# A four-layer attention and convolution kernel: symmetric layer 2 begins with its diagonal blocks, its closings are split into five parts, layer 1 is ticked at every step, end sums of layer 3 are recorded later

## The chip, the cores and the metric

The kernel runs on one core of a Trainium2 chip, as one program. The metric is the device time of one execution in microseconds (us). All data are fp32. The engines are named as in the profile: PE (TensorE matmul), PEld (its weight loads), DVE (VectorE), ACT (ScalarE), POOL (GpSimd), SP (SyncE, which here only issues DMAs).

## The reference, cut to what matters

The input x has shape (4, 64, 64, 64): four images of 64 by 64 pixels with 64 channels. Four layers follow one another, and every image passes all of them; only the normalisation at the end of layer 3 looks at all images together.

```python
x = L0(x)   # attention: softmax(q k^T) over 4096 tokens, out[n] = sum_m attn[m, n] v[m]; gamma * out + x
x = L1(x)   # layer norm, 64->256 pointwise, 3x3 depthwise, gate, mean over pixels, 128->64 pointwise, residual,
            # layer norm, 64->256 pointwise, gate, 128->64 pointwise, residual
x = L2(x)   # scores = X^T X over 4096 tokens (a symmetric matrix), softmax, product with X; + x
x = L3(x)   # attention with 32 inner channels, 1x1 projection, normalisation over all images; + x
```

## The kernel before, in words

**Layer 0** (`layer0`) has 32 items per image; an item is one tile of 128 tokens against all 4096. An item has four steps g. Each step records a score block (line 1090, eight matmul instructions), one exponential with its row sum on ACT (line 1095), and, six steps later (`LAG = 6`), a product block (line 1116, eight instructions). After step g = 0 of the next item `scale` (lines 1103 to 1106) makes the scaled weights `vq` on DVE that the products of the item need.

**Layer 1** (`layer1`, with `norm`) is a Python generator. Each `yield` hands back a number of lane microseconds; the class `Lane` advances its clock at every `tick` and records the generator's next part when the clock has passed what the parts before have asked for. So the layer's instructions are dealt out between the matmuls of other layers, and the order on every engine is the order in which they are recorded: PE, ACT, DVE and POOL keep that order strictly. There are two lanes, `conv` (layer 1) and `misc` (projections, closings, features). The depthwise convolution is 76 parts per image, nearly all DVE work (lines 1231 to 1244); the parts around it are matmuls (lines 1165, 1200, 1253, 1262, 1285) with ACT and DVE steps that wait for one another. Layer 1 of image b is handed to the lane at item 32 b + 34.

**Layer 2 of image 0** (`layer2`) has 32 items: four score blocks with exponentials (lines 1323, 1331), and one item later four product blocks (line 1341). `close2` scales the result and adds it to x (lines 1370 to 1377).

**Layer 2 of images 1 to 3** (`layer2s`) uses that the score matrix is symmetric. The 4096 tokens are cut into eight pieces of 512. Steps go over pairs (h, g) of pieces, 72 steps in all, two for each pair. A diagonal step (h = g, "own") has only a score block (line 1431), two exponentials (line 1436) and a product block (line 1481). Another step ("other") is also turned by DVE (line 1448, 32x32 block transposes), summed by POOL (line 1459), and, four turned steps at a time, multiplied again (`turned_products`, line 1497, 128 matmul instructions) and added to the accumulator `m.A` by DVE (line 1471). Step n is item n of the stage. A product block is recorded at least two items after its scores, none before item 4. The turned products of four steps follow two items after the last of them. `m.A` is allocated and cleared by POOL at one item. When the first half of the turned products of h = 6 has been recorded, `when_free` runs `keys3`, which copies the keys of layer 3 of the image before by 16 DMAs from SP (line 1620).

`close2s` finishes such an image: part 0 makes reciprocals of the sums (lines 1548 to 1554), then four parts each turn 1024 columns on PE (line 1559), scale them on DVE (line 1560) and add them to x (line 1566, two adds). It and `open3`, which makes the inputs of layer 3, run while the next image is in layer 2.

**Layer 3** (`layer3`) has 64 items in two halves of 32: scores (line 1641), two exponentials (line 1652), two items later products (line 1698) and a running sum of the exponentials in `m.tg`, two thirds on DVE (line 1689), one third by accumulating DMAs from POOL (line 1671, added at line 1691). `totals` sums over the partitions at the end of each half (matmul of line 1710), copies the sums (DVE, line 1734) and makes the reciprocals (ACT, lines 1718 and 1721, DVE lines 1726 to 1728).

**Order of stages.** Layer 0 of images 0 to 3 with layer 1 beside it, layer 2 of image 0, then for b = 1, 2, 3: layer 2 of image b (`layer2s(b)`) and layer 3 of image b - 1, and at the end layer 3 of image 3. The main loop `run` calls one item, ticks the lanes, runs what is due after this item (`at`), and ticks them again. Four slots of the PSUM tile `PS` are dealt out in turn; in `layer2s` three are, `new_ps()` each.

Of the kernel before, what the change touches and what calls it, by code (L numbers as in the profile page):

```python
# [691 lines left out]
def fast_path(ctx: ExitStack, tc: tile.TileContext, a: dict, out: bass.AP, bad):  # L692
# [387 lines left out]
    def layer0(b):  # L1080
        x, m = X[:, b], im[b]
        tiles = {}

        def score(t, g):
            es, _, zs = tiles[t]
            ps = new_ps()
            for c in range(2):
                for r in range(2):
                    rows_ = slice(64 * r, 64 * r + 64)
                    mm(  # L1090
                        ps[64 * c : 64 * c + 64, bass.ts(r, 512)],
                        m.q[rows_, 128 * t + 64 * c : 128 * t + 64 * c + 64],
                        x[rows_, bass.ts(g, 512)], start=True, stop=True,
                    )
            act(  # L1095
                es[g // 2][:, bass.ts(g % 2, 1024)], ps, AF.Exp, bias=SHIFT0,
                accum_out=zs[:, g : g + 1],
            )

        def scale(t):  # L1100
            _, vq, zs = tiles[t]
            tot = sums0[:, b, t : t + 1]
            nc.vector.tensor_reduce(tot, zs, AX.X, ALU.add)  # L1103
            rec = sm.tile([128, 1], F32, tag="rec", name="rec")
            nc.vector.reciprocal(rec, tot)
            nc.vector.tensor_scalar_mul(vq, m.v[:, t, :], rec)

        def product(t, i):
            if b == 0 and t == 0 and i == 0:
                take_slots(0, 1)  # L1110
            es, vq, _ = tiles[t]
            for s in range(2):
                for r in range(2):
                    j, rows_ = (i + 2 * r) % 4, slice(64 * r, 64 * r + 64)
                    k = 1024 * (j % 2) + 512 * s
                    ins = mm(  # L1116
                        PS[64 * s : 64 * s + 64, 2048 + 512 * j : 2560 + 512 * j], vq[rows_, :],
                        es[j // 2][rows_, k : k + 512],
                        start=t == 0 and i < 2, stop=t == 31 and i >= 2,
                    ).ins  # L1120
                    if s == r == 0 and len(steps) > 1:
                        wait_for(ins, steps[-2])
            steps.append(nc.gpsimd.nop(nofuse=True).ins)
            wait_for(steps[-1], ins)
            if t == 31 and i >= 2:
                for j in (i, i - 2) if b == B - 1 else (i - 2, i):
                    xs = x[:, bass.ts(j, 512)]
                    stt(xs, PS[:, 2048 + 512 * j : 2560 + 512 * j], gam0, xs, ALU.mult, ALU.add)
                if b == B - 1 and i == 3:
                    take_slots(0, 1, 2)  # L1130

        def item(t):
            tiles[t] = (
                [new_e() for _ in range(2)], sm.tile([128, C], F32, tag="vq", name="vq", bufs=4),
                sm.tile([128, 4], F32, tag="zs", name="zs", bufs=4),
            )
            for g in range(4):
                if g == 2 and between:
                    between.pop()()
                score(t, g)  # L1140
                late.append(lambda g=g: product(t, g))
                conv.tick(1.95)
                misc.tick(1.8)
                if g == 0 and t:
                    scale(t - 1)
                follow()
            if t == 31:
                scale(t)

        for t in range(32):  # L1150
            items.append((lambda t=t: item(t), 0.0))


    def norm(x, y):
# [2 lines left out]
        sq = [new_t("sq"), new_t("sq")]  # L1157
        for i in range(2):
            act(sq[i], x[:, bass.ts(i, 1024)], AF.Square)
        yield 3.0  # L1160
        ps = new_ps()
        for i, src in enumerate(((x, x), (sq[0], sq[1]))):
            for j in range(4):
# [30 lines left out]
    def layer1(b):  # L1194
# [53 lines left out]
                    yield 1.8  # L1248
        ytot = sm.tile([128, 1], F32, tag="ytot", name="ytot")
        nc.vector.tensor_reduce(ytot, ysum, AX.X, ALU.add)  # L1250
        yield 5.0
        ps = new_ps()
        mm(ps[:, 0:1], sca, ytot, start=True, stop=True)
        ch = sm.tile([128, 1], F32, tag="ch", name="ch")
# [18 lines left out]
        for j in range(4):  # L1273
            t, u = new_t(), new_t("u")
            for r in range(2):
# [3 lines left out]
                    act(t, ps, AF.Identity, bias=pwb[:, 1, 0:1])  # L1279
                else:  # L1280
                    stt(u, ps, pwb[:, 1, 1:2], t, ALU.add, ALU.mult)
                yield 4.0 if r else 3.0
            ps = new_ps()
            for s in range(2):
                mm(ps[64 * s : 64 * s + 64, 0:512], pw4, u[:, bass.ts(s, 512)], start=True, stop=True)
# [21 lines left out]
    def layer2(b):  # L1307
# [7 lines left out]
        def scores(n):  # L1315
# [3 lines left out]
            for jb in range(4 * (n % 8), 4 * (n % 8) + 4):  # L1319
# [10 lines left out]
                es[n, jb] = e[:, bass.ts(jb % 2, 1024)]  # L1330
                act(es[n, jb], ps, AF.Exp, bias=SHIFT2, accum_out=m.zs[:, jb, ib : ib + 1])  # L1331
                follow(0)

        def products(n):
            ib = n // 8
# [24 lines left out]
            )  # L1360

        for n in range(32):
            items.append((lambda n=n: scores(n), 4.6))
            at(first + n + (2 if n == 0 and b > 1 else 1), lambda n=n: products(n))
            if n % 8 == 7:
                at(first + n + 2, lambda n=n: turn(n // 8))
# [18 lines left out]
    def layer2s(b, when_free):  # L1385
# [2 lines left out]
        x, m, first = X[:, b], im[b], len(items)  # L1388
        xw = x.rearrange("p (w h) -> p w h", h=H)
        quads = ((0, 0), (1, 0), (0, 1), (1, 1))  # L1390
        m.zs = sm.tile([128, 144], F32, tag="zs2", name="zs2")
        m.cs = sm.tile([128, 128], F32, tag="cs2", name="cs2", bufs=1)
        used = {}
        steps = []
        for h in range(8):
            own = [(h, h, u, None, None) for u in range(2)]
            other = [
                (h, g, u, pi, 2 * gi + u)
                for pi, pair in enumerate(SIDES[h]) for gi, g in enumerate(sorted(pair)) for u in range(2)
            ]  # L1400
            steps += own + other if h < 6 else other + own
        st = {"e": {}, "T": {}, "esum": {}}

        def slot(g, t):
# [15 lines left out]
        def score(n):  # L1420
            h, g, u, pi, ti = steps[n]
            if n == 0:
                take_slots(0, 1, 2)
            if n % 2 == 0:
                st["pair"] = new_e()
            e = st["e"][n] = st["pair"][:, bass.ts(n % 2, 1024)]
# [34 lines left out]
                nc.gpsimd.tensor_add(esum[:, 0:512], esum[:, 0:512], esum[:, 512:1024])  # L1461

        def spread_sums(h):
            esum = st["esum"][h]
            nc.vector.transpose(esum[:, 512:1024], esum[:, 0:512])
            nc.vector.tensor_reduce(
# [22 lines left out]
        def turned_products(h, pi):  # L1489
            T, slots = st["T"][pi], [new_ps(), new_ps()]  # L1490
            for e in range(16):
                c = e % 2
                w = 1024 * (h % 2) + 256 * (e % 4) + 64 * (e // 4)
                for q in range(4):
# [3 lines left out]
                        slots[q // 2][64 * c : 64 * c + 64, o : o + 256], st["xr"][rows_, w : w + 64],  # L1498
                        T[rows_, bass.ts(e, 256)], start=e < 2, stop=e >= 14,
                    )  # L1500
            view = m.A.rearrange("p (g t q j) -> p g q t j", g=8, t=4, q=4)
            for i in range(2):
                for gi, g in enumerate(sorted(SIDES[h][pi])):
                    add_to(
                        view[:, g, 2 * i : 2 * i + 2],
                        slots[i].rearrange("p (q m) -> p q m", q=2)[:, :, 128 * gi : 128 * gi + 128]
                        .rearrange("p q (t j) -> p q t j", j=32),
                    )

        last_of = {}  # L1510
# [5 lines left out]
        def item(n):  # L1516
# [4 lines left out]
            turned(n)  # L1521
            column_sums(n)
            todo.append(n)
            if n == 6:
                m.A = new_big("A")
                nc.gpsimd.memset(m.A, 0.0)
            if n >= 4:
# [97 lines left out]
    def layer3(b):  # L1625
# [164 lines left out]
        for n in range(64):  # L1790
# [2 lines left out]
            if last and n == 63:  # L1793
                at(first + n + 2, close_last)
            elif n % 32 == 31:
                at(first + n + (2 if n == 63 and b < 2 else 4), lambda n=n: totals(n))
                at(first + n + 11, lambda n=n: close(n // 32))


# [10 lines left out]
    for b in range(B):  # L1810
# [4 lines left out]
            misc_from[f + 16] = [features2(b + 1)]  # L1815
        else:
            layer2s(b, lambda b=b: keys3(b - 1))
            misc_from[f + 3] = [close2(0) if b == 1 else close2s(b - 1)]
            misc_from[f + 28] = [open3(b - 1)]
            f = len(items)  # L1820
            misc_to[f] = True
            layer3(b - 1)
            if b + 1 < B:
                misc_from[f + 22] = [features2(b + 1)]
    f = len(items)

    def keys_of_last():
# [7 lines left out]
    def run():  # L1835
# [10 lines left out]
        for i in range(max(max(due) + 1, len(items))):  # L1846
# [7 lines left out]
            if i < len(items):  # L1854
                fn, us = items[i]
                fn()
            conv.tick(1.25 * us)
            misc.tick(us)
            for fn in due.get(i, []):
                fn()  # L1860
            conv.tick(1.25 * us)
            misc.tick(us)


# [183 lines left out]
```

## Time and profile before

| what | value |
| --- | --- |
| time, median of 3 runs | 2500.96 us (2496.73 to 2501.36) |
| time of the profiled execution | 2502.84 us |
| its span, first to last instruction | 2501.0 us |
| mean granted PE clock | 0.993 |
| PE busy | 2432.0 us (97%) |
| ACT busy | 1644.3 us (66%) |
| DVE busy | 1433.5 us (57%) |
| POOL busy | 506.7 us (20%) |

The stages as the trace shows them: layer 0 from about 18 to 1012 us; layer 2 of image 0 to about 1289 us; `layer2s(1)` to 1490 us, layer 3 of image 0 to 1629 us; `layer2s(2)` to 1832 us, layer 3 of image 1 to 1971 us; `layer2s(3)` to about 2175 us, and layer 3 of images 2 and 3 to about 2470 us; 31 us of output follow.

How to read it: the trace names each instruction by engine and source line. A timeline line gives start, duration, engine, line, operation, tiles, count, and in brackets the idle time before it with what ended it. A waits line reads "engine tile line <- releaser: us in total, times, longest us". A windows line gives a stretch, its length, busy us (instruction count) of PE, PEld, DVE, ACT and POOL, the granted PE clock, the DMA share and GB/s. Matmuls are pipelined, so a busy PE is not a PE at its peak: the number of instructions in a stretch says more than its busy time.

### The profile page before, as it was taken

The numbers are of one execution on the slowest core, as the hardware profiler recorded it, in microseconds if no ns is written. First come the engines' busy times: TensorE is split into PE (matmuls) and PEld (weight loads), VectorE is DVE, ScalarE is ACT, GpSimd is POOL, SyncE is SP. The second block draws the span as 40 slices with busy tenths as digits, with TensorE's granted clock in tenths as the row PEclk, the third lists the DMA queues.
The fourth block names the chain that finished last, engine by engine and source line by source line (L and its number), as shares of the span: only waits on it lengthen the run. The fifth ranks groups of instructions, "written<-read, shape, count | busy, mean of one in ns | idle before, by whom it ended". The sixth has DMA issues, their size and how long they took to land.

```text
span 2501.0 us, 62233 instructions
## 1 busy us (share of the span) xinstructions
PE 2432.0 (97%) x27037; PEld 937.0 (37%) x27037; DVE 1433.5 (57%) x1701; ACT 1644.3 (66%) x2975; POOL 506.7 (20%) x345
## 2 busy tenths in 40 slices
PE   9999999999999999999889999989999899999998
PEld 3343463334553446333224442134422245421113
DVE  2010267226652367258436657885668865687886
ACT  4666766666666776666554459944579744578996
POOL 2000000000000000000026651246731366511110
PEclk9999999999999999999999999999999999999999
DMA  3000000000000000010000017610066400275554
GB/s 78 1 18 1 18 1 18 18 18 2 18 1 18 18 18 1 18 18 18 18 18 19 19 45 152 136 27 19 19 128 128 85 19 21 60 152 119 119 119 120
DMA packets 59150, 115.33 MB, mean 46 GB/s; under 512 B 11148, under 2 KB 30325, under 8 KB 58869
## 3 DMA queue, kind: packets, MB, share of 16 engines
q0 software_dynamic: 19136, 67.68, 13.5%
q1 hardware_dynamic: 38981, 41.75, 7.5%
q8 instruction: 214, 3.51, 0.6%
q10 hardware_dynamic: 752, 1.85, 0.2%
q14 instruction: 67, 0.55, 0.1%
HBM read 4.80 MB, written 4.19 MB: 4 GB/s over the span
## 4 chain that ended last, share of the span: by engine, by line
PE 84%; DVE 9%; ACT 4%; DMA 1%; issue 1%; SPq 0%; DVEq 0%; POOL 0%; ACTq 0%; POOLq 0%
PE PS L1116 17%; PE PS L1090 17%; PE PS L1641 8%; PE PS L1431 7%; PE PS L1698 7%; PE PS L1481 7%; PE PS L1497 6%; DVE tg L1689 3%; PE PS L1341 3%; PE PS L1323 3%; PE PS L1200 2%; ACT e L1652 2%; DVE y L1233 2%; DMA xn<-e 1%; ACT e L1095 1%
## 5 line engine op out<-in xcount | busy, mean ns | idle before, releaser
L1095 ACT ACTIVATE e<-PS 128x1024 f32<-128x1024 f32 x512 | 523.7, 1023 | 326.3 <-PE PS L1090 285.4
L1116 PE MATMUL PS<-e,vq 64*64 64x512 f32 x4096 | 573.9, 591 | 0.0
L1090 PE MATMUL PS<-X,q 64*64 64x512 f32 x4096 | 571.4, 590 | 1.8 <-DVE X L974 1.7
L1652 ACT ACTIVATE e<-PS 128x512 f32<-128x512 f32 (+2 forms) x589 | 500.0, 919 | 53.0 <-PE PS L1641 29.9
L1436 ACT ACTIVATE e<-PS 128x512 f32<-128x512 f32 x432 | 253.6, 593 | 316.0 <-PE PS L1431 293.8
L1689 DVE TENSOR_TENSOR tg<-tg,e 128x2048 f32<-128x2048 f32 x174 | 398.5, 2290 | 51.7 <-ACT e L1652 39.8
L1459 POOL TENSOR_TENSOR esum<-e 128x1024 f32<-128x1024 f32 x21 | 49.7, 2367 | 1445.4 <-ACT e L1436 1445.4
L1233 DVE SCALAR_TENSOR_TENSOR y<-pad,vec,y 128x1024 f32<-128x1024 f32 x240 | 308.0, 1284 | 7.3
L1459 POOL TENSOR_TENSOR esum<-esum,e 128x1024 f32<-128x1024 f32 x126 | 299.1, 2374 | 52.3 <-ACT e L1436 44.9
L1641 PE MATMUL PS<-tg,ph 32*64 32x512 f32 x4096 | 299.2, 614 | 2.2 <-ACT e L1652 2.0
L1090 PEld LDWEIGHTS PS<-X,q 64*64 64x64 f32 x4096 | 195.0, 133 | 248.4 <-issue 166.0
L1116 PEld LDWEIGHTS PS<-e,vq 64*64 64x64 f32 x4096 | 195.3, 133 | 241.3 <-issue 141.3
L1698 PE MATMUL PS<-e,tg 128*32 128x512 f32 x2048 | 273.4, 606 | 0.0
L1448 DVE STREAM_TRANSPOSE turned<-e 128x1024 f32<-128x1024 f32 x168 | 206.6, 1239 | 69.4 <-ACT e L1436 69.2
L1431 PE MATMUL PS<-ko 64*64 64x512 f32 x1728 | 231.5, 601 | 3.9 <-DVE t L1560 3.9
L1481 PE MATMUL PS<-e,X 64*64 64x512 f32 x1728 | 223.6, 589 | 0.0
L1103 DVE TENSOR_REDUCE sums<-zs 128x1 f32<-128x4 f32 x128 | 19.8, 154 | 347.9 <-ACT e L1095 347.5
L1497 PE MATMUL PS<-turned,xn 32*64 32x256 f32 x5376 | 159.5, 381 | 15.1 <-DVE turned L1448 11.3
L1331 ACT ACTIVATE e<-PS 128x1024 f32<-128x1024 f32 x128 | 129.3, 1024 | 62.0 <-PE PS L1323 61.9
L1471 DVE TENSOR_TENSOR A<-PS,A 128x256 f32<-128x256 f32 (+1 forms) x216 | 92.4, 476 | 122.8 <-PE PS L1497 87.8
L1671 POOL DMA_DIRECT2D xn<-e x112 | 97.7, 910 | 291.1 <-ACT e L1652 208.5
L1641 PEld LDWEIGHTS PS<-tg,ph 32*64 32x64 f32 x4096 | 65.4, 130 | 224.2 <-ACT e L1652 174.5
(224 smaller groups left out, 1874.8 us busy)
## 6 DMA issues: line engine op xcount, KB each, us to landing
xn<-e POOLq DMA_DIRECT2D x128, 512.0 KB, 5.2
xn<-X SPq DMA_DIRECT2D x336, 32.0 KB
xn<-t SPq DMA_DIRECT2D x64, 128.0 KB
ph<-tg SPq DMA_DIRECT2D x64, 128.0 KB
ko<-ko SPq DMA_DIRECT2D x16, 256.0 KB
xr<-in_x_dram SPq DMA_DIRECT2D x13, 256.0 KB
q<-q SPq DMA_DIRECT2D x12, 256.0 KB
out_dram<-o SPq DMA_DIRECT2D x7, 256.0 KB
```

What stands on the lines that cost most here:

```text
L1090: mm(ps[64 * c : 64 * c + 64, bass.ts(r, 512)], m.q[rows_, 128 * t + 64 * c : 128 * t + 64 * c + 64], x[rows_, bass.ts(g, 512)], start=Tru ...
L1095: act(es[g // 2][:, bass.ts(g % 2, 1024)], ps, AF.Exp, bias=SHIFT0, accum_out=zs[:, g : g + 1],)
L1116: ins = mm(PS[64 * s : 64 * s + 64, 2048 + 512 * j : 2560 + 512 * j], vq[rows_, :], es[j // 2][rows_, k : k + 512], start=t == 0 and i < 2 ...
L1233: stt(y1, win, wt, y1, ALU.mult, ALU.add)
L1431: mm(ps[64 * c : 64 * c + 64, bass.ts(r, 512)], m.ko[rows_, k : k + 64], m.ko[rows_, bass.ts(h, 512)], start=True, stop=True,)
L1459: nc.gpsimd.tensor_add(esum, st["e"][n - 1] if (pi, ti) == (0, 1) else esum, st["e"][n])
L1481: mm(st["acc"][r][64 * c : 64 * c + 64, :], xw[rows_, jb, :], st["e"][n][rows_, bass.ts(c, 512)], start=n == mine[0], stop=n == mine[-1],)
L1497: mm(slots[q // 2][64 * c : 64 * c + 64, o : o + 256], st["xr"][rows_, w : w + 64], T[rows_, bass.ts(e, 256)], start=e < 2, stop=e >= 14,)
L1641: mm(PS[64 * c : 64 * c + 64, bass.ts(banks[k], 512)], m.ph[32 * k : 32 * k + 32, 128 * mc + 64 * c : 128 * mc + 64 * c + 64], m.th[32 * k ...
L1652: act(e[:, 512 * lo : 512 * k], PS[:, 512 * banks[lo] : 512 * banks[lo] + 512 * (k - lo)], AF.Exp,)
L1689: nc.vector.tensor_add(esum, esum, e)
L1698: mm(st["y"][32 * k : 32 * k + 32, :], m.gx[:, i % 32, :], es[i][:, bass.ts(k, 512)], start=mc == 0, stop=i % 32 == 31,)
```

## The change

1. Layer 0 ticks the conv lane by 2.3 instead of 1.95 at every step; in layer 2 of image 0 the lanes are ticked after each score block (2.3 and 1.8) instead of at the end of an item (four times 4.6, of which conv got 1.25 times as much). In the other stages conv no longer gets 1.25 times the item's time. Five pauses of layer 1 become longer.
2. `layer2s` takes h = 7, which has only diagonal steps, first, then h = 0 to 6; h = 6 alone ends with its diagonal steps. So the steps 0 to 3 and 70, 71 are diagonal. `m.A` is cleared at item 2 instead of 6; the tiles `zs` and `cs` are allocated when first used.
3. `close2s` is no longer dealt out by the misc lane from item 3 on, but one part each after the items 8, 12, 22, 32 and 42 of the next `layer2s`; `close2` starts at item 2 instead of 3, `open3` at 46 instead of 28, `features2` at item 3 instead of 22 of layer 3.
4. `totals` of the second half of layer 3 of images 0 and 1 is recorded five items after the last one instead of two, which is after item 4 instead of 1 of the next `layer2s`.
5. The view through which `turned_products` adds to `m.A` is written in another way, with the same addresses.

```diff
@@ layer0, item
-                conv.tick(1.95)
+                conv.tick(2.3)
                 misc.tick(1.8)
@@ norm
             act(sq[i], x[:, bass.ts(i, 1024)], AF.Square)
-        yield 3.0
+        yield 4.5
@@ layer1
         nc.vector.tensor_reduce(ytot, ysum, AX.X, ALU.add)
-        yield 5.0
+        yield 7.0
...
-                yield 4.0 if r else 3.0
+                yield 5.0 if r else 4.0
@@ layer2, scores, after each exponential
                 follow(0)
+                conv.tick(2.3)
+                misc.tick(1.8)
...
-            items.append((lambda n=n: scores(n), 4.6))
+            items.append((lambda n=n: scores(n), 0.0))
@@ layer2s
-        m.zs = sm.tile([128, 144], F32, tag="zs2", name="zs2")
-        m.cs = sm.tile([128, 128], F32, tag="cs2", name="cs2", bufs=1)
...
-        for h in range(8):
+        for h in (7, 0, 1, 2, 3, 4, 5, 6):
...
-            steps += own + other if h < 6 else other + own
+            steps += other + own if h == 6 else own + other
@@ layer2s, turned_products
-            view = m.A.rearrange("p (g t q j) -> p g q t j", g=8, t=4, q=4)
+            view = m.A.rearrange("p (g t q j) -> p q g t j", g=8, t=4, q=4)
...
@@ layer2s, item
-            if n == 6:
+            if n == 2:
                 m.A = new_big("A")
                 nc.gpsimd.memset(m.A, 0.0)
@@ layer3
-                at(first + n + (2 if n == 63 and b < 2 else 4), lambda n=n: totals(n))
+                at(first + n + (5 if n == 63 and b < 2 else 4), lambda n=n: totals(n))
@@ order of stages
             layer2s(b, lambda b=b: keys3(b - 1))
-            misc_from[f + 3] = [close2(0) if b == 1 else close2s(b - 1)]
-            misc_from[f + 28] = [open3(b - 1)]
+            if b == 1:
+                misc_from[f + 2] = [close2(0)]
+            else:
+                turns = close2s(b - 1)
+                for i in (8, 12, 22, 32, 42):
+                    at(f + i, lambda turns=turns: next(turns))
+            misc_from[f + 46] = [open3(b - 1)]
             f = len(items)
             misc_to[f] = True
             layer3(b - 1)
             if b + 1 < B:
-                misc_from[f + 22] = [features2(b + 1)]
+                misc_from[f + 3] = [features2(b + 1)]
@@ run
-            conv.tick(1.25 * us)
+            conv.tick(us)
             misc.tick(us)
             for fn in due.get(i, []):
                 fn()
-            conv.tick(1.25 * us)
+            conv.tick(us)
             misc.tick(us)
```

More of the change, by code (lines that the diff above doesn't have):

```diff
@@ L1423, in score @@
                 take_slots(0, 1, 2)
+                m.zs = sm.tile([128, 144], F32, tag="zs2", name="zs2")
             if n % 2 == 0:
@@ L1463, in spread_sums @@
         def spread_sums(h):
+            if h == 0:
+                m.cs = sm.tile([128, 128], F32, tag="cs2", name="cs2", bufs=1)
             esum = st["esum"][h]
@@ L1504, in turned_products @@
                     add_to(
-                        view[:, g, 2 * i : 2 * i + 2],
-                        slots[i].rearrange("p (q m) -> p q m", q=2)[:, :, 128 * gi : 128 * gi + 128]
-                        .rearrange("p q (t j) -> p q t j", j=32),
+                        view[:, 2 * i : 2 * i + 2, g],
+                        slots[i].rearrange("p (q g t j) -> p q g t j", q=2, g=4, t=4)[:, :, gi],
                     )
```

## The prediction

> **What bounds the kernel now.** The page first. PE is busy 97% of the span and holds 84% of the chain that ended last, so only time in which PE stands still or runs slowly can be won. I looked for it in the windows of 10 us.
>
> ```profile
> PE   9999999999999999999889999989999899999998
> 1300.00:1310.00 10.00, 6.23 (x60) 1.99 (x52) 9.86 (x7) 4.21 (x14) 9.77 (x5) 0.94 0.03 8
> 1310.00:1320.00 10.00, 2.45 (x48) 2.45 (x55) 9.68 (x9) 0.00 (x0) 5.79 (x2) 0.50 0.01 2
> 1330.00:1340.00 10.00, 10.00 (x192) 4.97 (x188) 5.29 (x8) 4.80 (x16) 3.84 (x3) 1.00 0.10 25
> 1630.00:1640.00 10.00, 6.93 (x47) 1.28 (x50) 7.57 (x4) 3.11 (x10) 0.00 (x0) 0.82 0.21 54
> 1200.00:1210.00 10.00, 6.60 (x62) 2.58 (x62) 8.24 (x12) 3.34 (x7) 0.00 (x0) 0.99 0.00 0
> ```
>
> The first two windows are the start of `layer2s(1)`: PE issues little, DVE is busy 9.7 and more of 10 us. The third is the same stage in its stride. The fourth is the start of `layer2s(2)`, the last the end of layer 1 of image 3 in layer 2 of image 0. Then the waits of PE, by what ended them, and the timeline there:
>
> ```profile
> PE PS L1497 <- DVE turned L1448: 11.3, 1, 11.3
> PE PS L1710 <- DVE tg L1689: 10.8, 6, 3.0
> PE PS L1253 <- DVE ytot L1250: 3.4, 1, 3.4
> ```
>
> ```profile
> 1302.30 2.72 DVE L1377 TENSOR_TENSOR X<-X,ph 128x512 f32<-128x512 f32 x1
> ...
> 1312.30 0.69 DVE L1377 TENSOR_TENSOR X<-X,ph 128x512 f32<-128x512 f32 x1
> ...
> 1317.55 6.16 PE L1497 MATMUL PS<-turned,xn 32*64 32x256 f32 x128 [11.32 <-DVE turned L1448]
> ...
> 1627.64 9.48 DVE L1689 TENSOR_TENSOR tg<-tg,e 128x2048 f32<-128x2048 f32 x4
> ...
> 1637.17 1.93 PE L1710 MATMUL PS<-tg,ones 128*32 128x512 f32 x8 [3.05 <-DVE tg L1689]
> ...
> 1661.06 3.70 PE L1497 MATMUL PS<-turned,xn 32*64 32x256 f32 x124 [2.12 <-DVE t L1560]
> ```
>
> In image 1 the closing of image 0 (lines 1375, 1377) stands in front of the transposes on DVE, and PE waits for those 11.32 us. In image 2 the end sums of layer 3 (line 1710) stand in front of everything on PE while DVE still has four adds; then ACT idles 4.98 us for the copy of the sums, and the closing delays the transposes to 1661.
>
> **The change part by part.** The sum is made against the profiled execution (2502.84 us, 1.9 above the median of the runs, 1.8 above its span). PE's price in stride: 32 matmuls of line 1341 take 3.43 us, so a score or product block of eight takes 0.86; the 128 of line 1497 take 3.64.
>
> *Starts of `layer2s`.* From the first scores to the end of the first turned products:
> - Image 2: 1628.94 to 1664.69, 35.75 us. PE's work in it: 8 score blocks 6.9, 6 product blocks 5.1, line 1497 3.6, two blocks of line 1698 1.7, line 1710 0.9, four of line 1559 4.4, line 1548 0.3; together 22.9. Lost: 12.9.
> - Image 3, the same list, 1971.17 to 2005.55: 34.4, lost 11.5.
> - Image 1, 1289.23 to 1323.63: 34.4, less 6.9, 5.1, 3.6, one product item of layer 2 3.4 and 0.5 for line 1354; lost 14.9.
>
> After the change the steps 0 to 3 need no DVE. Image 2, walked through: scores 2 to 4 follow the last product block of layer 3 (1634.1) at once; PE comes to line 1710 about 1638.5, when DVE has ended its adds (1637.1); the first turned products come at item 9, after ten score and eight product blocks, at about 1649, and the fourth transpose is done about then (ACT needs 1.58 per step: 2 x 593 + 2 x 199 ns). By 1652.7 PE has done 22.2 us of work in 23.8. The 1.3 us that the first scores wait for a bank (2.17 instead of 0.86) stay, and ACT, now 1.58 behind each step, costs another 1.5. I leave 3 us in images 2 and 3: gain 9.9 and 8.5. Image 1: `close2` runs in items 2 and 3, before the first transpose. DVE has about 0.24 + 0.35 + 4 x (0.65 + 0.69) = 6 us to do from 1296.5, then four transposes of 1.24 after the exponential of step 4 (about 1301): ready near 1309, and PE comes there at 1309.5. That is a close meeting; I leave 2 us: gain 12.9. Bounds for the three together: 23 (every meeting missed by 2 to 3 us) to 36.
>
> The adds of line 1377 took 2.72 while POOL summed (1301.8 to 1310.0) and 0.69 during its memset (1309.94 to 1313.44), so the memset, which now falls beside `close2`, costs DVE nothing. [...]
>
> *Closings after items 8, 12, 22, 32, 42.* The PE work is the same. DVE: 1.2 + 2 x 1.0 us per part (means of lines 1560, 1566; 1.0 holds some waiting for POOL), put where two diagonal steps leave out 2 x 1.24 of transposes. In stride DVE is busy about 6.3 of 10 us, so 1 us too much is caught up before the next turned products, seven items on. Cover gone: one wait of up to 2.5 us per part. I take +1.5 over both images (0 to +5). The PSUM slot of a part comes back after DVE's 1.2 us; PE meets it again after two blocks (1.7).
>
> *Ends of `layer2s`.* The second turned products of h = 6 move from item 69 to 71, next to layer 3. Its first scores want two slots that DVE must empty first: two adds of 0.42 per slot, about 1 us, in three images: +3 (0 to +5). `keys3` follows the first turned products of h = 6; from there to the first scores of layer 3 it was 14.3 us (1475.87 to 1490.13) and is now four score and product pairs and 3.64, 10.5 us. SP issues its 16 DMAs in 10.96 us, but the first scores read only the columns of the first four, about 3 us of issuing: nothing. Should they wait for all 16, 1 to 3 us each; that is in the +5. `open3` and `features2` are moved whole, with their DMAs (SP, idle there); in layer 3 `features2` no longer puts two DVE copies of 1.22 before the crowded end of the first half, where PE waited 1.8 for line 1710: -3 over two images (0 to -5).
>
> *Layer 2 of image 0.* Counting instructions in windows of 24 us at the prices above, 1012 to 1300 lost 18 us: 4.4 at 1060 to 1084 and 7.2 at 1204 to 1228 (the wait for `ytot` and a clock of 0.84), the rest in small pieces. Before, layer 1 of image 2 reached into it up to item 134. By the lane's arithmetic it now ends at item 128, image 3 gets 9.2 lane us per item instead of 11.5, and its depthwise parts spread over 14.9 items instead of 11.9: 102 us of PE for 95 of DVE, so DVE has no lag left when `ytot` is wanted. The squares of `norm` still come one score block before their matmuls: 1.5 us of stall each, and some for line 1285. The last `pw4` falls on item 1 of `layer2s(1)`. Gain 9 (4 to 14).
>
> *Layer 0.* Here the tick costs. DVE's depthwise parts are (308.0 + 25.8 + 22.6 + 20.8 + 2.6) / 4 = 95 us per image, in 76 parts of 1.8. Per item of four steps (6.87 us of PE) the lane now advances 9.2: 14.9 items, 102 us of PE; DVE needs 95 + 14.9 x 0.57 (`scale`) = 103.5. Before it was 17.5 items, 120 us for 105:
>
> ```profile
> 306.00:356.00 50.00, 50.00 (x471) 32.54 (x465) 40.80 (x56) 32.32 (x58) 0.00 (x0) 1.00 0.01 1
> DVE sums L1103 <- ACT e L1095: 10.3, 6, 4.6
> ```
>
> The 10.3 us idle of these 50 are what the faster tick eats. What is queued behind a late part on DVE is `scale`, and for it PE's product waits, recorded two steps (3.4 us) later. An overload of 1.3 us per image, in two pieces, fits into that: +2.5 (-1 to +12). PE's moved layer 1 work is neutral: in full stride in both stages.
>
> Sum: -31.3 + 1.5 + 3 - 3 - 9 + 2.5 = -36.3, so 2466.5 for an execution like the profiled one (2464.7 from the median; the two are within the spread of the runs, and I keep the first).
>
> The clock: the 128 matmuls after the 11.32 us took 6.16 instead of 3.64 at a clock of 0.50, which is inside the 14.9. At image 2 a wait of 3.05 us went with 0.82 and 0.84 for 20 us, at image 3 the same wait with 1.00; that is the 1.4 between them. [...]
>
> **Rivals.**
> 1. *The backlog moves.* DVE does the same work, and the close meetings at item 9 and the closings beside POOL are missed: half of the starts' gain (16) goes, and the closings cost their 5 instead of 1.5: 2466.5 + 16 + 3.5 = 2486. For it: 9.7 of 10 us DVE busy at the starts. Against: four steps less of transposes there.
> 2. *Slower: DVE becomes the bound in layer 0.* If its wait for the exponentials (10.3 us in 7.3 items, 1.4 per item) does not vanish when DVE is late, an item of the convolution needs 103.5 / 14.9 + 1.4 = 8.35 us instead of 6.87; 1.48 x 44.7 items = 66, net 2502.8 - 38.8 + 66 = 2530. It decides from 38.8 / 44.7 = 0.87 us per item on. Against: a late DVE finds its exponential finished.
> 3. *No change.* The starts win little because ACT's 1.58 per step takes over: 2498. Against: ACT's busy share there is below 0.5.
>
> **How the numbers follow.** Forecast 0.70, rival 1 0.18, rival 2 0.07, rival 3 0.05. The measurement tells 0.2% (5 us) from no change. The forecast's unknowns reach from 2447 (36, 14, -1, ends at zero, 5 for layer 3) to 2485 (23, 4, some cost in layer 0); with rival 1, 2451 to 2488 leaves out two in ten. Faster 0.90, same 0.04, slower 0.06.
>
> **What would show it.** Right: the wait of line 1497 for line 1448 is below 2 us, line 1710 no longer waits at the two starts, the stretch to the first turned products is shorter by about 10 at images 2 and 3 net of the four closings, layer 2 of image 0 is shorter by more than its moved work. Layer 0 ends no later than the moved 12 to 16 us of matmuls explain. Wrong: PEld waits for `vq` in layer 0, or line 1497 waits behind line 1560 or 1566 at items 13, 23, 33, 43.

## The result and the profile after

The changed kernel takes 2475.11 us (median of 4 runs, 2472.05 to 2475.64) against 2501.16 before: ratio 0.9897, 95% interval [0.988, 0.9914]. A second set beside a later group of experiments gave 2472.97 (4 runs), ratio 0.989 [0.9875, 0.9906]. The profiled execution took 2475.64 us (span 2473.9) against 2502.84 (span 2501.0). So the change is faster by 26 us (28 in the second set), as forecast in sign, about 10 us less than the forecast's 36. The forecast's sum hides two errors of opposite sign, and the experiments gave a third correction: what makes the starts of images 2 and 3 shorter is mostly not the order of the steps.

Line numbers shift: 1431 is now 1432, 1448 is 1449, 1459 is 1460, 1471 is 1474, 1481 is 1484, 1497 is 1500, 1375 and 1377 are 1377 and 1379, 1548 to 1566 are 1550 to 1568, and from 1641 on two are added.

First PE's line of the page and the windows that answer to those of before: start of `layer2s(1)` (two), start of `layer2s(2)`, and layer 2 of image 0. The columns are the length, busy us (instructions) of PE, PEld, DVE, ACT and POOL, the granted clock, DMA share and GB/s.

```profile
PE   9999999999999999999989999999999999999998
1290.00:1300.00 10.00, 5.94 (x32) 2.09 (x36) 5.85 (x5) 0.23 (x1) 1.72 (x1) 0.66 0.18 44
1300.00:1310.00 10.00, 10.00 (x191) 5.12 (x187) 5.54 (x6) 4.83 (x16) 8.59 (x4) 1.00 0.02 4
1630.00:1640.00 10.00, 8.76 (x174) 4.49 (x171) 7.64 (x14) 2.65 (x9) 9.38 (x4) 1.00 0.07 16
1200.00:1210.00 10.00, 10.00 (x76) 2.75 (x76) 2.08 (x3) 6.04 (x12) 0.00 (x0) 1.00 0.00 0
```

Of the four 8s that PE's line had inside the span one is left. It is the start of image 1: in the first window PE issues 32 matmuls in 10 us, the clock falls to 0.66, and DVE, the limit there before, is busy only 5.85 us. In the window of layer 2 of image 0 (last line) PE is now busy 10.00 of 10 us, where it was 6.60. PE's waits name what took the place of the 11.3 us for line 1448:

```profile
PE PS L1484 <- DVE A L1474: 6.1, 1, 6.1
PE PS L1643 <- DVE A L1474: 3.3, 3, 1.5
PE PS L1712 <- DVE tg L1691: 2.2, 4, 0.6
PE PS L1500 <- DVE sums L1554: 1.6, 2, 0.8
```

The turned products (1500) wait for no transpose any more, and the end sums (1712) wait 2.2 us in all instead of 10.8. New are 6.07 us in one place, and 1.1 us on average at the three ends of `layer2s`. The timeline of the start of image 1 shows who holds whom:

```profile
1285.23 1.90 PE L1484 MATMUL PS<-e,X 64*64 64x512 f32 x16
...
1288.23 0.69 DVE L1379 TENSOR_TENSOR X<-X,ph 128x512 f32<-128x512 f32 x1
...
1289.39 2.34 POOL L1460 TENSOR_TENSOR esum<-e 128x1024 f32<-128x1024 f32 x1 [256.40 <-ACT e L1437]
...
1289.56 2.71 DVE L1379 TENSOR_TENSOR X<-X,ph 128x512 f32<-128x512 f32 x1
1292.19 1.23 DVE L1449 STREAM_TRANSPOSE turned<-e 128x1024 f32<-128x1024 f32 x1
1293.36 1.44 DVE L1474 TENSOR_TENSOR A<-PS,A 128x512 f32<-128x512 f32 x2
1294.06 4.48 PE L1484 MATMUL PS<-e,X 64*64 64x512 f32 x16 [6.07 <-DVE A L1474]
...
1299.77 0.60 ACT L1437 ACTIVATE e<-PS 128x512 f32<-128x512 f32 x1 [10.46 <-PE PS L1432]
...
1305.66 3.71 PE L1500 MATMUL PS<-turned,xn 32*64 32x256 f32 x128
```

The product blocks of h = 7 (line 1484, 1285.23) fill the two accumulator banks of PSUM. The next product block belongs to h = 0 and needs the same banks, which DVE empties at line 1474. On DVE that stands behind the whole of `close2` and one transpose, so it starts at 1293.36. PE stands still for 6.07 us and ACT for 10.46 us, and of the four transposes that were to come early the third has to wait for ACT until 1301.07. The turned products then come at 1305.66 with no wait for a transpose: the meeting that the prediction worked out was not missed by DVE, because PE itself came late.

The same view at the start of image 2, where nothing of the kind happens:

```profile
1620.98 1.06 PE L1712 MATMUL PS<-tg,ones 128*32 128x512 f32 x8
...
1624.53 0.72 ACT L1720 ACTIVATE inv<-yz 128x256 f32<-128x256 f32 x2 [3.28 <-DVE yz L1736]
...
1635.11 3.70 PE L1500 MATMUL PS<-turned,xn 32*64 32x256 f32 x124 [0.79 <-DVE sums L1554]
```

The end sums go through without a wait; part 0 of the closing holds the turned products for 0.79 us.

By stages, from the first and last matmuls of each (us):

| stage | before | after | moved |
| --- | --- | --- | --- |
| up to the first scores of `layer2s(1)` | 1289.2 | 1274.3 | -14.9 |
| `layer2s(1)`, `(2)`, `(3)` to the first scores of layer 3 | 200.9, 203.4, 202.0 | 199.5, 197.1, 197.1 | -1.4, -6.3, -4.9 |
| of that, start to end of the first turned products | 34.5, 35.8, 34.4 | 35.1, 27.4, 27.4 | +0.6, -8.4, -7.0 |
| layer 3 of image 0, of image 1 | 138.8, 138.8 | 137.6, 138.0 | -1.2, -0.8 |
| layer 3 of images 2 and 3 | 291.9 | 294.3 | +2.4 |

The stretches to the first turned products (below: the starts) don't hold the same matmuls. With the new order they hold two score and two product blocks more, 3.4 us; at images 2 and 3 they no longer hold the four turns of line 1559 (1561 after the change), 4.4 us; at image 1 1.9 us of layer 1 have come in. Where two kernels differ in the order, the whole of `layer2s` is the fair comparison.

### The profile page after: what moved, and what is told of

Read it like the earlier page. It is cut to its first block, busy times and chain, and to the rows that moved or that the text cites. A ratio compares the mean times of both kernels' runs of the same rounds, so it can differ in the third digit from the quotient of the medians.

```text
span 2473.9 us, 62215 instructions
## 1 busy us (share of the span) xinstructions
PE 2431.5 (98%) x27037; PEld 925.5 (37%) x27037; DVE 1428.7 (58%) x1701; ACT 1642.7 (66%) x2979; POOL 506.8 (20%) x345
## 4 chain that ended last, share of the span: by engine, by line
PE 88%; DVE 5%; ACT 4%; DMA 1%; issue 1%; SPq 0%; POOL 0%; DVEq 0%; ACTq 0%; POOLq 0%
PE PS L1116 18%; PE PS L1090 17%; PE PS L1643 8%; PE PS L1700 8%; PE PS L1432 7%; PE PS L1484 7%; PE PS L1500 6%; PE PS L1323 4%; PE PS L1343 4%; PE PS L1200 2%; DVE tg L1691 2%; ACT e L1654 2%; DMA xn<-e 1%; ACT e L1095 1%; PE PS L1165 1%
## 5 line engine op out<-in xcount | busy, mean ns | idle before, releaser
L1090 PEld LDWEIGHTS PS<-X,q 64*64 64x64 f32 x4096 | 184.4, 133 | 257.3 <-issue 178.8
L1116 PEld LDWEIGHTS PS<-e,vq 64*64 64x64 f32 x4096 | 184.6, 133 | 251.3 <-issue 152.9
L1484 PE MATMUL PS<-e,X 64*64 64x512 f32 x1728 | 232.7, 594 | 6.2 <-DVE A L1474 6.1
L1528 POOL MEMSET A<- 128x4096 f32 x3 | 11.2, 3736 | 1012.5 <-PE PS L1116 1012.5
```

What stands on the lines that cost most here:

```text
L1090: mm(ps[64 * c : 64 * c + 64, bass.ts(r, 512)], m.q[rows_, 128 * t + 64 * c : 128 * t + 64 * c + 64], x[rows_, bass.ts(g, 512)], start=Tru ...
L1116: ins = mm(PS[64 * s : 64 * s + 64, 2048 + 512 * j : 2560 + 512 * j], vq[rows_, :], es[j // 2][rows_, k : k + 512], start=t == 0 and i < 2 ...
L1484: mm(st["acc"][r][64 * c : 64 * c + 64, :], xw[rows_, jb, :], st["e"][n][rows_, bass.ts(c, 512)], start=n == mine[0], stop=n == mine[-1],)
```

## Experiments

Two groups of questions: what the wait at image 1 costs and what makes it, and which part of the change earns what. All were timed in 5 rounds against the kernel before; a ratio is to that kernel, "against the changed kernel" means its 2475.1 or 2473.0.

**e1, a later `close2`.**

```diff
-                misc_from[f + 2] = [close2(0)]
+                turns = close2(0)
+                for i in (12, 22, 32, 42):
+                    at(f + i, lambda turns=turns: next(turns))
```

> The changed kernel, but the four parts of close2 (image 0) come after items 12, 22, 32 and 42 of layer2s(1), like those of images 1 and 2, instead of items 2 and 3. Theory A: image 1's start gave back its gain because the products of h = 0 need the two accumulator banks that DVE must first empty (line 1474 for h = 7), and on DVE those adds stand behind the eight instructions of close2. Then the wait of line 1484 for line 1474 (6.07 us, clock 0.66 after it) goes, first scores to end of first turned products in image 1 goes from 35.0 to about 27, and the time falls by 6 to 8 us to about 2468. Rival B: beginning with h = 7 is itself too quick a change of accumulators, whatever DVE has in front; then the wait stays above 3 us and the time within 2 us of 2475.

2464.97 us (2462.67 to 2467.94), ratio 0.985 [0.9836, 0.9865], 10 less than the first set of the changed kernel. The wait of line 1484 shrinks to 1.2 us, and the start of image 1 takes 28.2 instead of 35.1 us. So the wait is caused by `close2` ahead of line 1474, and it is worth more than its own length: 4.9 us of it go and the start is 6.9 us shorter, as the slow matmuls behind the wait go too (the longest of line 1484 takes 0.64 us in e1, 1.11 in the changed kernel).

**e2, other engines empty the banks.** `close2` stays early; only the accumulators of h = 7 no longer go through DVE.

```diff
-                for r in range(2):
-                    add_to(m.A[:, bass.ts(h, 512)], st["acc"][r])
+                cols = m.A[:, bass.ts(h, 512)]
+                if h == 7:
+                    half_ = new_e("half")[:, 0:512]
+                    nc.scalar.copy(cols, st["acc"][0])
+                    nc.scalar.copy(half_, st["acc"][1])
+                    nc.gpsimd.tensor_add(cols, cols, half_)
+                else:
+                    for r in range(2):
+                        add_to(cols, st["acc"][r])
```

> The changed kernel, but the accumulators of h = 7 are emptied by ACT (two copies of 128x512) and summed by POOL, instead of by two DVE adds; close2 stays in items 2 and 3. Theory A (the banks behind close2 on DVE): the wait of line 1484 falls from 6.07 to below 1, the first turned products of image 1 end some 5 us sooner, time about 2470. Rival C (DVE simply has too much to do there, and the accumulators are only where it shows): the wait moves on to line 1500 for the transposes of line 1449, 3 us or more, and the time stays within 2 us of 2475.

2461.68 us (2461.2 to 2463.34), ratio 0.9838 [0.9825, 0.9851]. Its timeline at the same place:

```profile
1286.28 0.58 ACT L1492 COPY A<-PS 128x512 f32<-128x512 f32 x1
1286.76 0.59 ACT L1493 COPY half<-PS 128x512 f32<-128x512 f32 x1
...
1289.68 2.73 DVE L1379 TENSOR_TENSOR X<-X,ph 128x512 f32<-128x512 f32 x1
...
1292.34 6.87 DVE L1449 STREAM_TRANSPOSE turned<-e 128x1024 f32<-128x1024 f32 x6
...
1297.01 3.93 PE L1507 MATMUL PS<-turned,xn 32*64 32x256 f32 x128 [0.79 <-DVE turned L1449]
```

The banks are free 14.1 us after the first scores of the stage (1286.76 + 0.59, less 1273.3), in the changed kernel after 20.5 (1293.36 + 1.44, less 1274.3). DVE is as late as there, its last add still takes 2.73 us, and it costs PE 0.79 us. Two different edits that have only the banks in common take the wait away and make `layer2s(1)` 6.9 and 7.5 us shorter: that settles the cause. The whole time falls by more, 10 and 13 us against the first set (8 and 11 against the second). In e2, emptying h = 7 this way also shortens the starts of images 2 and 3 from 27.4 to 26.0, 2.8 us together; in e1's profile 3.1 us lie in layer 3 of images 2 and 3, which varies by itself (see e11).

**e3, layer 1's ticks as before.** Part 1 of the change undone (the five pauses, the ticks of layer 0, of layer 2 of image 0 and of `run`).

```diff
-                conv.tick(2.3)
+                conv.tick(1.95)
...
-        yield 4.5
+        yield 3.0
...
-        yield 7.0
+        yield 5.0
...
-                yield 5.0 if r else 4.0
+                yield 4.0 if r else 3.0
...
-                conv.tick(2.3)
-                misc.tick(1.8)
...
-            items.append((lambda n=n: scores(n), 0.0))
+            items.append((lambda n=n: scores(n), 4.6))
...
-            conv.tick(us)
+            conv.tick(1.25 * us)
```

> The changed kernel with part 1 of the change undone: ticks of 1.95 in layer 0, lanes ticked at the end of an item in layer 2 of image 0, 1.25 times the item's time for conv, the short pauses of layer 1. By the two traces (layer 2 of image 0 loses 18 us before and 3 after, layer 0 4 and 7, and 2.5 us of layer 1 spill into layer2s(1)) the time rises by about 10, to 2485. By the terms of the prediction (9 less 2.5) it rises by 6.5, to 2482. Rival: the finer ticking did nothing and the gain came from the later stages: 2475.

2482.73 us (2479.34 to 2484.8), ratio 0.9919 [0.9905, 0.9934]: +7.6 against the changed kernel. Three old waits of layer 1 come back:

```profile
PE PS L1285 <- DVE u L1281: 4.4, 3, 1.5
PE PS L1253 <- DVE ytot L1250: 3.4, 1, 3.4
PE PS L1165 <- ACT sq L1159: 3.2, 2, 1.6
```

The start of `layer2s(1)` is 13.5 us later than in the changed kernel (1287.8), but that stage is 4.7 us shorter: none of layer 1 is left over into it (1.9 us of matmuls), and PE's wait for the emptied banks is 3.2 instead of 6.1 us. The edit undoes the finer ticks and the longer pauses together; no run tells them apart. The ticks earn more than the time shows: a part is spent again at image 1.

**e4, the old order of the pieces**, with the closings one or two items earlier so that they still fall on diagonal steps.

```diff
-        for h in (7, 0, 1, 2, 3, 4, 5, 6):
+        for h in range(8):
-            steps += other + own if h == 6 else own + other
+            steps += own + other if h < 6 else other + own
-            if n == 2:
+            if n == 6:
-                for i in (8, 12, 22, 32, 42):
+                for i in (6, 10, 20, 30, 40):
```

> The changed kernel with the old order of layer2s (h = 0 to 7, m.A cleared at item 6; the closings after items 6, 10, 20, 30, 40, which are the diagonal steps of that order), everything else as changed. Theory A with the traces: at image 1 the wait for the accumulators (6) goes and the wait of the first turned products for DVE (11.3 before) comes back for the most part, net +2 to +5; images 2 and 3 lose 1 to 3 each because the transposes start two items earlier; time 2479 to 2486. Rival: the split closings and the late end sums carry all the gain and the order none: within 2 us of 2475.

2477.57 us (2476.02 to 2480.08), ratio 0.9903 [0.9887, 0.9919]: +2.5, within the uncertainty. At image 1 the old wait is back:

```profile
PE PS L1500 <- DVE turned L1449: 12.4, 1, 12.4
PE PS L1712 <- DVE tg L1691: 1.7, 3, 0.6
```

At images 2 and 3 line 1500 starts 1.8 us late each (0.45 in the changed kernel); the profile names no releaser, but it starts just as a transpose of line 1449 ends that stood on DVE behind the end sums' last step (2.72 us). The starts of images 2 and 3 take 25.9 and 24.2 us. That is less than the 27.4 with the new order, but those hold 3.4 us more matmuls; for the same work the old order is 1.9 and 0.2 us slower, and `layer2s` as a whole says the same: 198.8 and 197.1 against 197.1 twice. So in images 2 and 3 the diagonal steps first account for at most 2 of the 6.3 and 4.9 us that the stages gained.

**e5, the end sums as before.**

```diff
-                at(first + n + (5 if n == 63 and b < 2 else 4), lambda n=n: totals(n))
+                at(first + n + (2 if n == 63 and b < 2 else 4), lambda n=n: totals(n))
```

> The end sums of layer 3 of images 0 and 1 go back to two items after its last item, with all else as after the change. Theory (the late end sums free PE and ACT at the starts of images 2 and 3): line 1712 waits about 3 us again for line 1691 at two starts, ACT idles about 5 us for the copy of the sums, and each stretch from the first scores to the end of the first turned products grows from 27.4 to 31 to 33 us; 7 to 11 us slower than the changed kernel, 2482 to 2486. Rival (with diagonal steps first, nothing there needs DVE before item 9, so only PE's own wait counts): 2 to 4 us slower, about 2478.

2478.11 us (2477.58 to 2480.44), ratio 0.9906 [0.9891, 0.9921]: +3.0. The wait and ACT's idle time are those of the profile before:

```profile
1618.06 1.94 PE L1712 MATMUL PS<-tg,ones 128*32 128x512 f32 x8 [3.05 <-DVE tg L1691]
...
1620.79 0.72 ACT L1720 ACTIVATE inv<-yz 128x256 f32<-128x256 f32 x2 [4.98 <-DVE yz L1736]
...
1627.49 2.31 PE L1484 MATMUL PS<-e,X 64*64 64x512 f32 x13 [1.63 <-DVE A L1474]
```

The starts grow to 31.5 and 31.9 us as the theory said, 8.6 together, yet the time by 3.0 only (5.1 against the second set). In the two profiled executions the rest is in layer 3 of images 2 and 3 (290.2 us here, 294.3 there) and 1.0 before `layer2s(1)`; see e11.

**e6, the closings dealt out by the lane again.**

```diff
-                turns = close2s(b - 1)
-                for i in (8, 12, 22, 32, 42):
-                    at(f + i, lambda turns=turns: next(turns))
+                misc_from[f + 3] = [close2s(b - 1)]
```

> The closings of images 1 and 2 are again dealt out by the misc lane from item 3 of the next layer2s on; the rest is as after the change. Theory (it is the five parts that keep DVE free for the first turned products): the lane puts the parts one after another among the first 15 or so items, line 1500 waits again 3 us or more in each of the two images, 5 to 9 us slower than the changed kernel, about 2482. Rival (diagonal steps first leave DVE so much room that the place of the closing no longer matters): within 2 us of the changed kernel.

2489.61 us (2487.34 to 2493.85), ratio 0.9951 [0.9937, 0.9966]: +14.5, the largest of all parts, and more than either theory said. The starts of images 2 and 3 take 41.1 and 41.2 us, longer than before the change even less the 3.4 us of added blocks, and `layer2s(2)` and `(3)` 206.1 us each against 203.4 and 202.0. PE's waits and the place:

```profile
PE PS L1432 <- DVE t L1562: 11.6, 4, 4.5
PE PS L1500 <- DVE turned L1449: 5.4, 2, 2.7
```

```profile
1627.90 2.70 DVE L1730 SCALAR_TENSOR_TENSOR yz<-inv,yz 128x512 f32<-128x512 f32 x1
1630.70 1.23 DVE L1562 TENSOR_TENSOR t<-PS,rz 128x1024 f32<-128x1024 f32 x1
...
1631.98 1.99 PE L1432 MATMUL PS<-ko 64*64 64x512 f32 x8 [4.53 <-DVE t L1562]
```

A part of the closing has turned its columns into a PSUM slot and must wait on DVE behind the arithmetic that follows the end sums; the scores want that slot and wait 4.53 us. Then the four transposes queue behind the closing as before.

**e7, `features2` at item 22 again.**

```diff
-                misc_from[f + 3] = [features2(b + 1)]
+                misc_from[f + 22] = [features2(b + 1)]
```

> features2 of the images 2 and 3 goes back to item 22 of layer 3 of images 0 and 1, with all else as after the change. The prediction gave its move 3 us in two images; by that 2478. Rival (the two copies of 1.2 us on DVE are hidden anyway): within 1 us of the changed kernel.

2475.48 us (2472.53 to 2477.87), ratio 0.9896 [0.988, 0.9911]. In the time there is no difference. In its profile layer 3 of images 0 and 1 takes 138.4 and 138.9 us instead of 137.6 and 138.0, and line 1712 waits 4.7 instead of 2.2 us: 1.7 us in the two stages, too little for the runs to tell.

**e9, the old order with a late `close2`**, e4's edit and this one: is the order worth something once no closing is in the way at all?

```diff
-                misc_from[f + 2] = [close2(0)]
+                turns = close2(0)
+                for i in (10, 20, 30, 40):
+                    at(f + i, lambda turns=turns: next(turns))
```

> The old order of the pieces (h = 0 to 7, the memset at item 6, the later closings after items 6, 10, 20, 30, 40) together with a close2 in four parts after items 10, 20, 30, 40. It asks what the new order is worth once no closing stands ahead of the first turned products in any image; the kernel to compare is e1, 2465.0. Theory now (the order by itself is worth little): the start of image 1 takes 25 to 28 us as in e1 (28.3), layer2s 193 to 199 us, the time is within 3 us of e1. Rival (the diagonal steps first are what makes room for the transposes): line 1500 waits several us for line 1449 at image 1, 2470 or more.

2467.13 us (2463.79 to 2467.44), ratio 0.986 [0.9845, 0.9875], 2.2 more than e1. With the old order the start of image 1 is even shorter (22.5 against 28.2 us, of which 3.4 are the blocks that it doesn't hold), as line 1474 isn't needed before h = 1; `layer2s(1)` is 1.8 us shorter, `layer2s(2)` and `(3)` are 2.9 and 2.8 us longer (200.0 and 199.9). So the order by itself is worth about 2 us in the times, no more than the runs can tell, and 4 to 5 us in the three stages (590.7 against 586.9 us here, 598.9 against 593.7 for e4).

**e10, the old order and the old closings**: the first three pairs of lines of e4's edit, and this.

```diff
-                turns = close2s(b - 1)
-                for i in (8, 12, 22, 32, 42):
-                    at(f + i, lambda turns=turns: next(turns))
+                misc_from[f + 3] = [close2s(b - 1)]
```

> The old order and the old closings of images 1 and 2 together; layer 1's ticks, the late end sums, features2 and close2 as after the change. e6 alone was 2489.6, e4 alone 2477.6, the changed kernel 2475.1. If the two edits add up, 2492. If, as I think, the diagonal steps at items 0 to 3 only let the lane's closing in ahead of everything else on DVE and PE's slots wait for it (4.5 us in e6), the old order with the old closings is better than e6: starts of images 2 and 3 of 31 to 36 us instead of 41.2, 2478 to 2486.

2489.88 us (2488.36 to 2493.96), ratio 0.996 [0.9947, 0.9974]. I expected the old order to bear the lane's closing better, 2478 to 2486; it does not. Line 1432 waits for line 1562 as in e6:

```profile
PE PS L1500 <- DVE turned L1449: 12.4, 1, 12.4
PE PS L1432 <- DVE t L1562: 11.6, 2, 5.8
```

The closings are worth 12 to 17 us with either order (e6 and e10 against the changed kernel and e4). And the late end sums alone gain nothing: here they are late, and the starts of images 2 and 3, with the same matmuls as before the change, take 36.7 and 38.3 us, before 35.8 and 34.4. They pay only once the closing is out of their way.

**e11, the changed kernel again.**

> The changed kernel itself once more, beside the others on the same chip: 2475 within 3 us. Of its layer 3 of images 2 and 3, which took 294.3 us in its first profile and 289.3 to 292.2 in those of the experiments with the same code there, I expect 289 to 292 if the 294.3 belong to that one execution, 294 again if they belong to the changed kernel.

2472.97 us, 2470.98 in its profile, with layer 3 of images 2 and 3 in 289.2 us. The 294.3 belonged to the one execution: in it line 1643 waited 2.48 us at 2222 us, and from 2224 to 2231 the granted clock was 0.51 and PE issued 34 matmuls, where e11 issued 80; 16 of line 1643 took 2.01 us, in e11 1.11. Over all profiles that stage goes from 288.1 to 294.3 us. So the +2.4 of the table is no effect of the change, and single profiles can be compared stage by stage but not in their sum.

**e8, a better version**: e1 and e2 together, and part 0 of the later closings after item 10 instead of 8.

```diff
-                for i in (8, 12, 22, 32, 42):
+                for i in (10, 12, 22, 32, 42):
```

> A version made from the two experiments that were faster: close2 in four parts after items 12, 22, 32, 42 of layer2s(1), the last accumulators of layer 2 of image 0 emptied by two copies on ACT and an add on POOL, and part 0 of the later closings after item 10 instead of 8. If both edits only remove the same wait of line 1484, as I think, the start of image 1 cannot be won twice: 26 to 27.5 us there instead of 27.6, and the time is that of the ACT copies alone, 2460 to 2462, less up to 1.5 us for the waits of line 1500 for line 1554 at images 2 and 3. If the late close2 also spares DVE beside the POOL sums, 2457 or less.

2458.24 us (2457.2 to 2459.49), ratio 0.9827 [0.9813, 0.9841], the fastest of all: 15 to 17 us less than the changed kernel. The starts take 26.5, 24.7 and 24.7 us. It is 3.4 us less than e2: in the profiles `layer2s` is 1.1 us shorter in each image, at images 2 and 3 mostly because the waits for line 1554 (0.8 us each) are gone. What is left of PE's waits between 1270 and 2140 us is small:

```profile
PE PS L1650 <- DVE A L1474: 3.3, 3, 1.5
PE PS L1719 <- DVE tg L1698: 1.1, 2, 0.5
PE PS L1507 <- DVE turned L1449: 1.0, 2, 0.5
```

## Why the prediction was right or wrong

| term | predicted | measured | from |
| --- | --- | --- | --- |
| start, image 1 | -12.9 | about -4 | stage -1.4, less 1.1 (its end) and 1.9 (layer 1 left over) |
| starts, images 2, 3 | -9.9, -8.5 | about -8.2, -6.8 | stages -6.3, -4.9, less 1.1 and 0.8 (part 0) each |
| closings at diagonal steps | +1.5 | +1.6 | wait for line 1554 |
| ends of `layer2s` | +3 | +3.3 | wait of line 1643 for line 1474 |
| layer 3 of images 0, 1 | -3 | -2.0 | stages; 1.7 by e7 |
| layer 2 of image 0 | -9 | about -15 | lost time 18 to 2.9 |
| layer 0 | +2.5 | about +3 | lost time 3.9 to 7.0 |

The lost times are counted in the same way before and after: length of the stage less the matmuls in it at their spacing in stride.

**The step that failed** is image 1's start, in the sentence "after the change the steps 0 to 3 need no DVE". They do: h = 7 has two diagonal steps, so its banks must be emptied after two product blocks, by two adds on DVE, and the prediction had `close2` on DVE at just that time. It counted the queue in front of the transposes and overlooked the queue in front of line 1474. Before, pieces of 0 to 6 had other steps as well and the banks changed hands later. e1 and e2 show the price in that stage: 6.9 and 7.5 us. The 1.9 us of layer 1 that fall into this stage (8 matmuls of line 1200 and 4 of line 1285) it saw coming only in part ("the last `pw4` falls on item 1"). In the same passage ACT's price per step is misread: the 0.2 us rows that read the sums overlap the next exponential. Without a wait ACT starts one every 0.57 us (1284.33, 1284.90, 1285.47 after the change), so a step of two takes 1.14 us and not 1.58, and the third rival's ground was weaker than it was put.

**The term that was too small** is layer 2 of image 0. The prediction let the squares' stalls and some of line 1285 stay. They went: after the change PE has no wait for lines 1281 and 1250 and 0.4 us for the squares (line 1159), and e3 brings back 11.0 us of them (4.4 + 3.4 + 3.2). The prediction counted the lane's advance and not that the longer pauses leave these steps more time; that the pauses did it, and not the ticks, is likely but not shown. The two errors, +9 and -6, largely cancel, and that the time came out this near is in part luck.

**Right sum, wrong reason**: at images 2 and 3 the sizes held to 2 us, but the prediction laid them to the diagonal steps first and the later line 1710. Undoing one part at a time costs, against the first set of the changed kernel: closings 14.5, ticks 7.6, late end sums 3.0, order 2.5, `features2` 0.4; against the second set each is 2.1 more. That they add up to 28 or 39 us, where the whole is 26 to 28, shows that they are not shares of one sum. The closings and the late end sums work together: `layer2s(2)` and `(3)` take 405.5 us before, 409.9 with the late end sums alone (e10), 402.8 with the split closings and the new order but not the late end sums (e5), 395.9 with split closings and late end sums in the old order (e4), 394.2 with all three. The order, which the change is named after first, is one of the smallest parts. For the closings the prediction had only a cost (+1.5, right), and their gain was hidden in the starts.

**The rivals.** Rival 1 named the right kind of thing, a close meeting on DVE behind the closing, but for the wrong reader (line 1500) and with half of the starts' gain lost where it was two fifths (12 of 31). Rival 2 (DVE bound in layer 0, 2530) did not come: PE never waits for `vq`. PEld does before line 1116, 0.8 us in three waits that it did not have before, and layer 0 ends 17.8 us later, 14.7 of them moved matmuls and 3.1 lost. Rival 3 is out. Of the signs that were to show it, three held (line 1500 no wait for 1449, line 1712 free at the starts, layer 2 of image 0 shorter by more than its moved work). Two did not quite: the stretches at images 2 and 3 are 8.4 and 7.0 shorter instead of about 10, and layer 0 ends 1.8 us later than the 12 to 16 us allowed for. The sign of being wrong, PEld waiting for `vq`, came too, but small.

## What to carry to other kernels

When steps are put first because they don't need a busy engine, go through everything they hold as well as what they read: a short first group hands on its accumulator banks sooner, and whoever empties them must not stand behind the work you meant to get away from. Undo the parts of a change one by one before crediting the one it is named after: here the closings, spread to places where DVE has room, and the end sums moved late earned most at images 2 and 3, and the end sums only because the closing was out of their way. Such single prices don't add up where parts lean on each other, and two stretches can be compared only after counting the work in them. A forecast that comes out near the time can still have two wrong terms; compare it term by term.

## What the runs showed of the hardware

In some windows with a wait of PE the granted clock was lower, and the work behind the wait took longer. With the 6.07 us wait the clock of the window from 1290 to 1300 us was 0.66, and 16 matmuls of line 1484 took 4.48 us, 1.90 just before. Behind the 4.53 us of e6 eight matmuls of line 1432 took 1.99 us instead of 1.09; what clock they had is not shown. With the 2.48 us wait in layer 3 after the change the clock was 0.51 for 7 us. Not every such wait showed it: of two waits of 3.05 us before the change one went with 0.82, the other with 1.00.

The adds of line 1379 (1377 before), which DVE makes from two SBUF inputs, took 2.71 to 2.73 us beside a POOL sum of line 1460 (1459 before; 2.34 to 2.80 us each) and 0.69 alone, in the kernels before, after and e2, while the transposes of line 1449, with one input, took 1.25 beside sums of that line. How many adds met a sum differed with the place: three of the four of `close2` before the change, one after it. In e1, where `close2` is late, all four took 1.65 us and the four scalings of line 1377 1.98 to 2.65 instead of 0.69, 11 us more of DVE time, and the kernel was 10 us faster: here it was worth more to keep the work out of PE's way than its longer time cost.
